# Attention outputs divided in the transposed layout, with reciprocals spread by DMA through HBM

## The chip, the cores and the metric

The kernel runs on one core of a Trainium2 chip. A core has a matrix engine (TensorE, "PE" in the profile; its weight loads are listed as "PEld"), three engines for elementwise work (VectorE "DVE", ScalarE "ACT", GpSimd "POOL"), a queue engine that only issues transfers (SyncE "SP"), and 16 DMA engines that carry the transfers. Each engine works through its own list of instructions in order, and waits at semaphores for the others. The metric is the device time of one execution in microseconds; lower is better. The median of three runs is compared.

## The reference

The input is x of 8 images x 512 tokens x 512 features, float32. The block is a half feed-forward, an attention, and a half feed-forward again, each on a layer-normalised input and added to x:

```python
x = x + 0.5 * ffn(layernorm(x), w_gate_up, w_proj)
x = x + attn(layernorm(x), Wq, Wk, Wv, Wo)
x = x + 0.5 * ffn(layernorm(x), w_gate_up, w_proj)
```

The feed-forward computes `silu(gate) * up` with ternary weights, normalises by the root mean square, and projects back. The attention has 32 heads of 16 features, and a sliding window: a query in a block of 128 tokens sees the keys of its own block and of the block before, at most 128 tokens back:

```python
scores = einsum('bhnrd,bhncd->bhnrc', qb, kw) * scale
scores = where(valid, scores, finfo(float32).min)
out = einsum('bhnrc,bhncd->bhnrd', softmax(scores), vw)
return out.reshape(B, T, D) @ Wo.T
```

The softmax's division can be done after the weighting: weight the values by the exponentials, sum the exponentials too, and divide the one by the other. The change is about where and in which layout this division is done.

## The kernel before

Three stages follow one another: the first feed-forward (tensors named `_a`), the attention (`_b`), the second feed-forward (`_c`). Intermediate rows go through HBM (`rows_a`, `rows_b`). SBUF memory of the attention is reused by the last stage's tiles, so some loads of its weights (`wgu`, `wp`) wait until attention tiles are released.

**The attention stage** (line 610 on). An image is cut in 4 chunks of 8 heads (`i` counts chunks over all images, 32 in all, `NJ` = 4 per image), and a chunk in 4 units of 128 tokens (`u` counts units, `t` is the unit in its chunk, 0 to 3). One pass of the loop at line 902 emits the work of one unit, in an order written out by hand for TensorE, VectorE, ScalarE and GpSimd; the order of SyncE's transfers is left to the scheduler. In a pass:

- `probabilities(u)`: scores in transposed form, keys on partitions (tile `sp`, line 798), turned into exponentials by ScalarE with one part on VectorE (lines 806 to 812, tile `pT`), and masked by GpSimd (line 817).
- `weighted(u - 1)`: the weighting (tile `av`, line 833). It needs the mask of the unit before. Its stationary operand is `vones`: for every head 32 columns, 16 of them the values, 16 of them ones. So `av` has, for each head, 16 rows of weighted values (numerators) and 16 rows that all hold the sum of the exponentials (denominators), in the transposed layout: features on partitions, tokens along the free dimension. There are 4 heads side by side in the 128 partitions, and two such halves `h`.
- `maxima(u + 6)`: scores in the other form (tile `sm`, line 750) and their row maxima on VectorE (line 758).
- projections, one per unit: values of the next image at t = 0 (`wv`), output of the last image at t = 1 (`wo`, `output(b - 1, j)`), queries and keys of chunk i + 3 at t = 2 and t = 3 (`wq`, `wk`). The query and key terms are rearranged over partitions by four transfers each on SyncE (lines 708 and 720).
- the division, every second unit, for two units together: ScalarE copies `av` to SBUF (tile `ab`, line 842); `turned` transposes it on TensorE (tile `abT`, line 851), tokens onto partitions; `divided` takes reciprocals of the denominators and multiplies on VectorE (lines 857 and 861, tile `o`); `turned_back`, one unit later, transposes back on TensorE (tile `oTp`, line 873), and ScalarE copies the result into `oT` (line 876), from which the output projection reads.

Pools set what can be in flight: `ps_s` has 6 PSUM buffers for scores and transposes, `ps_av` one and `ps_mm` one, `work` and `opool` hold the SBUF tiles.

Of the kernel before, what the change touches and what calls it, by code (L numbers as in the profile page):

```python
# [8 lines left out]
F32 = mybir.dt.float32  # L9
# [6 lines left out]
P = 128  # L16
# [8 lines left out]
def macaron_block(  # L25
# [63 lines left out]
    h_kept = [dram.tile([P, T], F32, name=f"h_kept{c}") for c in range(FC)]  # L89
    wp_kept = [dram.tile([P, 2, D], F32, name=f"wp_kept{u}") for u in range(FC // 2)]  # L90
# [519 lines left out]
    def attention_stage():  # L610
# [19 lines left out]
        opool = pool(s, "o_b", 7)  # L630
# [15 lines left out]
        for name, src in (("wv", wv_t), ("wq", wq_t), ("wk", wk_t), ("wo", wo_t)):  # L646
            attn_w[name] = fixed[name].tile([P, DC, D], F32, name=f"{name}_sb")
            nc.sync.dma_start(attn_w[name], src.rearrange("(c p) e -> p c e", p=P))
# [11 lines left out]
        for tile_ in vones:  # L660
            nc.gpsimd.memset(tile_[:, :, :, DK:], 1.0)
# [4 lines left out]
        abTs, qs, ks, ms, pTs, avs, abs_, os_, oTs = {}, {}, {}, {}, {}, {}, {}, {}, {}  # L666
# [57 lines left out]
        def values(b, t):  # L724
            rows = slice(t * P, (t + 1) * P)
            pairs = [(xss[b][:, k, rows], attn_w["wv"][:, k, :]) for k in range(DC)]
            sum_of_products(
                f"wv_{b}_{t}", pairs,
                lambda ps: nc.vector.tensor_copy(
                    vones[b % 2][:, t, :, :DK], ps.rearrange("p (h d) -> p h d", d=DK)  # L730
                ),
            )
# [90 lines left out]
        def weighted(u):  # L823
# [16 lines left out]
            if t % 2 == 1:  # L840
                abs_[i] = work.tile([P, 2, 2, P], F32, tag="ab", name=f"ab_{u}", bufs=2)
                nc.scalar.copy(abs_[i], avs.pop(i))

        def turned(u):

            i, t = u // TB, u % TB
            pt = abTs[i] = ps_s.tile([P, 2, 2, P], F32, tag="s", name=f"abT_{u}")
            ab = abs_.pop(i)
            for m in range(2):
                for h in range(2):  # L850
                    nc.tensor.transpose(pt[:, m, h, :], ab[:, h, m, :], ident)  # L851

        def divided(u):
            i, t = u // TB, u % TB
            rows = abTs.pop(i).rearrange("p m h (g r) -> p (m h) g r", r=32)
            rden = small.tile([P, 4, NG, 1], F32, tag="rden", name=f"rden_{u}")
            nc.vector.reciprocal(rden, rows[:, :, :, DK : DK + 1])
            os_[i] = work.tile([P, 2, 2, NG, DK], F32, tag="o", name=f"o_{u}", bufs=2)
            for m in range(2):
                for h in range(2):  # L860
                    nc.vector.tensor_tensor(
                        os_[i][:, m, h], rows[:, 2 * m + h, :, :DK],
                        rden[:, 2 * m + h].to_broadcast([P, NG, DK]), ALU.mult,
                    )

        def turned_back(u):
            i, t = u // TB, u % TB
            if t == 1:
                oTs[i] = opool.tile([P, T], F32, tag="oT", name=f"oT_{i}")
            o = os_.pop(i)  # L870
            back = ps_s.tile([P, 2, P], F32, tag="s", name=f"oTp_{u}")
            for m in range(2):
                nc.tensor.transpose(
                    back[:, m, :], o[:, m].rearrange("p h g d -> p (h g d)"), ident
                )
            nc.scalar.copy(
                oTs[i][:, (t - 1) * P : (t + 1) * P], back.rearrange("p m q -> p (m q)")
            )
# [23 lines left out]
        for u in range(-row - row // 2 - 2, units + row):  # L902
# [13 lines left out]
            if t == 0 and 0 <= b - 1 < B:  # L916
                residual_loaded(b - 1, j)
# [15 lines left out]
            if t == 1 and 0 <= b - 1 < B:  # L933
                output(b - 1, j)
# [46 lines left out]
```

## Time and profile before

| | |
|---|---|
| median of 3 runs | 2475.7 us (2471.64 to 2480.78) |
| span of the profiled execution | 2475.1 us (the page gives no time of its own around it; the median is 0.6 us above) |
| attention stage in the span | about 800 to 1730 us |
| one image of it, 4 chunks | 109 us |
| mean granted TensorE clock | 0.977 of full speed |
| `abT` transposes on TensorE | 256 matmul records (1% of the chain that ended last) |
| `oTp` transposes on TensorE | 128 matmul records |
| HBM read, written | 66.32 MB, 41.16 MB |

A line of the profile names the source line, the engine, the operation, what is written and read, the number of instructions, and the time. A bracket behind a line of the list in order of time is the idle time of the engine just ahead, and who ended it. "SPq" lines are the times in which SyncE issues transfers, not the transfers themselves; these have their own table of times from issue to landing. The granted clock is the share of full speed at which TensorE was allowed to run; 1.00 is full speed.

### The profile page before, as it was taken

The numbers are of one execution on the slowest core, as the hardware profiler recorded it, in microseconds if no ns is written. First come the engines' busy times: TensorE is split into PE (matmuls) and PEld (weight loads), VectorE is DVE, ScalarE is ACT, GpSimd is POOL, SyncE is SP. The second block draws the span as 40 slices with busy tenths as digits, with TensorE's granted clock in tenths as the row PEclk, the third lists the DMA queues.
The fourth block names the chain that finished last, engine by engine and source line by source line (L and its number), as shares of the span: only waits on it lengthen the run. The fifth ranks groups of instructions, "written<-read, shape, count | busy, mean of one in ns | idle before, by whom it ended". The sixth has DMA issues, their size and how long they took to land.

```text
span 2475.1 us, 43237 instructions
## 1 busy us (share of the span) xinstructions
PE 2387.1 (96%) x17208; PEld 1779.4 (72%) x17208; DVE 1339.8 (54%) x3929; ACT 982.2 (40%) x1476; POOL 862.8 (35%) x714
## 2 busy tenths in 40 slices
PE   5999999999999999999999999987899999999998
PEld 4778888888887456666666666654688888888887
DVE  7884444453444666766767676662444443453442
ACT  6773222222221355656566565654222222222221
POOL 0000444444445122223222223222345444444444
PEclk9899999999999989999999999988899999999999
DMA  4443100000011523333332333253100000000000
GB/s 161 145 145 129 42 35 1 34 35 1 35 52 34 145 53 87 101 79 88 81 105 74 93 81 83 74 166 125 68 35 1 35 35 1 35 34 1 35 17 17
DMA packets 63192, 160.58 MB, mean 65 GB/s; under 512 B 7440, under 2 KB 11536, under 8 KB 59920
## 3 DMA queue, kind: packets, MB, share of 16 engines
q1 hardware_dynamic: 47680, 116.68, 16.5%
q10 hardware_dynamic: 15312, 41.16, 4.4%
q8 instruction: 135, 2.21, 0.4%
q14 instruction: 65, 0.53, 0.1%
HBM read 66.32 MB, written 41.16 MB: 43 GB/s over the span
## 4 chain that ended last, share of the span: by engine, by line
PE 92%; DVE 3%; ACT 2%; issue 1%; DMA 0%; POOL 0%; ACTq 0%; POOLq 0%; DVEq 0%; SPq 0%
PE gu_c L281 19%; PE gu_a L281 18%; PE o_c L316 9%; PE o_a L316 9%; PE sp L798 5%; PE av L833 5%; PE wk L677 5%; PE wv L677 5%; PE wq L677 5%; PE wo L677 5%; PE sm L750 4%; PE abT L851 1%; PE neg L777 1%; PE ptn_b L225 1%; PE ptn_a L225 1%
## 5 line engine op out<-in xcount | busy, mean ns | idle before, releaser
L281 PE MATMUL gu_a<-xs_a,wgu_a 128*128 128x512 f32 x2048 | 497.8, 396 | 7.2 <-ACT sg_a L292 3.0
L281 PE MATMUL gu_c<-xs_c,wgu_c 128*128 128x512 f32 x2048 | 490.4, 392 | 0.7 <-ACT xs_c L228 0.7
L817 POOL TENSOR_SCALAR_AFFINE_SELECT pT<-pT 128x1024 f32<-128x1024 f32 x224 | 243.2, 1106 | 632.9 <-ACT pT L812 632.9
L281 PEld LDWEIGHTS gu_a<-xs_a,wgu_a 128*128 128x128 f32 x2048 | 387.2, 191 | 90.7 <-ACT sg_a L292 4.3
L281 PEld LDWEIGHTS gu_c<-xs_c,wgu_c 128*128 128x128 f32 x2048 | 383.3, 189 | 80.1 <-ACT xs_c L228 1.1
L758 DVE CUSTOM_DVE_ANT_0 seen<-sm,window 128x256 f32<-128x256 f32 (+1 forms) x1024 | 331.3, 387 | 86.6 <-PE sm L750 85.9
L316 PE MATMUL o_a<-wp_a,hs_a 128*128 128x512 f32 x1024 | 256.3, 395 | 0.0
L316 PE MATMUL o_c<-wp_c,hs_c 128*128 128x512 f32 x1024 | 251.6, 389 | 0.0
L297 DVE TENSOR_TENSOR h_c<-gu_c,sg_c 128x512 f32<-128x512 f32 x128 | 88.2, 689 | 276.8 <-PE gu_c L281 274.5
L587 POOL TENSOR_TENSOR sq_c<-h_c 128x512 f32<-128x512 f32 x120 | 125.0, 1042 | 316.4 <-DVE h_c L297 301.6
L810 ACT ACTIVATE pT<-sp 128x512 f32<-128x512 f32 (+1 forms) x384 | 181.2, 545 | 129.3 <-PE sp L798 129.3
L812 ACT ACTIVATE pT<-pT 128x2048 f32<-128x2048 f32 (+1 forms) x128 | 217.3, 1697 | 10.9 <-DVE pT L806 7.6
L316 PEld LDWEIGHTS o_a<-wp_a,hs_a 128*128 128x128 f32 x1024 | 192.7, 190 | 40.0 <-DVE hs_a L306 0.4
L316 PEld LDWEIGHTS o_c<-wp_c,hs_c 128*128 128x128 f32 x1024 | 192.2, 188 | 39.9
L297 DVE TENSOR_TENSOR h_a<-gu_a,sg_a 128x512 f32<-128x512 f32 x128 | 88.2, 689 | 234.7 <-PE gu_a L281 230.0
L588 POOL TENSOR_TENSOR ss_c<-ss_c,sq_c 128x512 f32<-128x512 f32 x120 | 192.2, 1602 | 8.9
L292 ACT ACTIVATE sg_c<-gu_c 128x512 f32<-128x512 f32 x128 | 76.6, 599 | 261.3 <-PE gu_c L281 248.2
L302 ACT CAST hs_c<-h_c 128x512 fp32r<-128x512 f32 x128 | 79.4, 621 | 252.7 <-DVE h_c L297 252.7
L587 POOL TENSOR_TENSOR sq_a<-h_a 128x512 f32<-128x512 f32 x90 | 94.2, 1047 | 229.7 <-DVE h_a L297 220.7
L306 DVE TENSOR_TENSOR hs_c<-h_c,hs_c 128x512 fp32r<-128x512 f32 x128 | 124.1, 970 | 83.1 <-ACT hs_c L302 83.1
L292 ACT ACTIVATE sg_a<-gu_a 128x512 f32<-128x512 f32 x128 | 76.4, 597 | 214.8 <-PE gu_a L281 203.2
L302 ACT CAST hs_a<-h_a 128x512 fp32r<-128x512 f32 x115 | 71.3, 620 | 202.0 <-DVE h_a L297 199.6
(137 smaller groups left out, 3129.1 us busy)
## 6 DMA issues: line engine op xcount, KB each, us to landing
ks<-k SPq DMA_DIRECT2D x128, 256.0 KB, 4.8
qs<-q SPq DMA_DIRECT2D x128, 128.0 KB, 2.4
wf_gu<-w_gate_up_dram SPq DMA_DIRECT2D x16, 512.0 KB, 3.6
wgu_kept<-wgu_a ACTq DMA_DIRECT2D x16, 512.0 KB, 2.7
rows_a<-x_a ACTq DMA_DIRECT2D x8, 1024.0 KB, 4.0
x_b<-rows_a SPq DMA_DIRECT2D x8, 1024.0 KB, 5.5
xr<-rows_a ACTq DMA_DIRECT2D x32, 256.0 KB, 5.4
rows_b<-xr SPq DMA_DIRECT2D x32, 256.0 KB, 2.1
```

The lines of the kernel that those rows point to most:

```text
L281: nc.tensor.matmul(ps, wgu[c][:, i * DC + k, :], xss[b][:, part, k, :], start=(k == 0 and part == 0), stop=(k == DC - 1 and part == 1),)
L292: nc.scalar.activation(sg, gate, AF.Silu)
L297: nc.vector.tensor_tensor(h, up, sg, ALU.mult)
L302: nc.scalar.copy(hs[:, 0, :], h)
L316: nc.tensor.matmul(ops[t], hs[:, part, t * P : (t + 1) * P], wp[e // 2][:, e % 2, :], start=(e == begin and part == 0), stop=(e == end and ...
L587: nc.gpsimd.tensor_tensor(sq, h, h, ALU.mult)
L588: nc.gpsimd.tensor_tensor(sumsq, sumsq, sq, ALU.add)
L677: nc.tensor.matmul(ps, lhs, rhs, start=(n == 0), stop=(n == len(pairs) - 1))
L758: nc.vector.tensor_tensor_reduce(out=seen[:, : n * P], in0=tiles[g][:, h, : n * P], in1=window[:, (2 - n) * P :], scale=-1.0, scalar=3.4e3 ...
L810: nc.scalar.activation(under, tiles[g][:, :, : n * P], AF.Relu, scale=-1.0)
L812: nc.scalar.activation(seen, seen, AF.Exp, scale=-1.0)
L817: nc.gpsimd.affine_select(out=half, in_=half, compare_op=ALU.is_ge, fill=0.0, base=0, pattern=[[0, 2 * NG], [sign, P]], channel_multiplier ...
```

## The change

Nothing is transposed any more for the division; it is done in the layout that the weighting leaves.

- For heads with `h` = 0 the values stand in the even columns of `vones` and ones in the odd ones; for `h` = 1 the other way round. So numerators and denominators alternate over partitions. `values` writes the columns by two copies, and the memset covers the whole of `vones`.
- ScalarE copies `av` into `sums` (the copy of line 842, a tile over the whole chunk).
- At t = 0 of the next chunk, `denominators` stores one denominator row per head to HBM (two transfers) and loads them back as 128 partitions x 32 (one transfer); `gathered` copies the numerators of `h` = 1 over the denominators of `h` = 0 (one transfer), so that one tile holds all numerators.
- At t = 2, `inverted` takes reciprocals on VectorE, stores them to HBM (one transfer) and reads every row back onto the 16 partitions of its head (eight transfers). All of these are on SyncE's queue.
- At t = 3, `divided` multiplies on GpSimd, into `oT`.
- The output projection and its residual load come one chunk later, the loop runs four units longer, `oT` has 8 buffers instead of 7, and `wo` is loaded with its rows interleaved, by two transfers.

```diff
--- before.py
+++ after.py
@@ -87,6 +87,8 @@
     rows_b = [dram.tile([P, TB, D], F32, name=f"rows_b{b}") for b in range(B)]
     wgu_kept = [dram.tile([P, 2 * DC, P], F32, name=f"wgu_kept{c}") for c in range(FC)]
     h_kept = [dram.tile([P, T], F32, name=f"h_kept{c}") for c in range(FC)]
+    dens = [dram.tile([2, NG, T], F32, name=f"dens{n}") for n in range(2)]
+    inverses = [dram.tile([2, NG, T], F32, name=f"inverses{n}") for n in range(2)]
     wp_kept = [dram.tile([P, 2, D], F32, name=f"wp_kept{u}") for u in range(FC // 2)]
 
     PSUM = bass.MemoryType.PSUM
@@ -627,7 +629,7 @@
         }
         ring = pool(s, "ring_b", 3)
         probs = pool(s, "probs_b", 3)
-        opool = pool(s, "o_b", 7)
+        opool = pool(s, "o_b", 8)
         work = pool(s, "work_b", 3)
 
         ps_s = pool(s, "ps_s", 6, PSUM)
@@ -645,7 +647,14 @@
         attn_w = {}
         for name, src in (("wv", wv_t), ("wq", wq_t), ("wk", wk_t), ("wo", wo_t)):
             attn_w[name] = fixed[name].tile([P, DC, D], F32, name=f"{name}_sb")
-            nc.sync.dma_start(attn_w[name], src.rearrange("(c p) e -> p c e", p=P))
+            if name != "wo":
+                nc.sync.dma_start(attn_w[name], src.rearrange("(c p) e -> p c e", p=P))
+                continue
+            by_half = src.rearrange("(c h r) e -> h r c e", h=2, r=P // 2)
+            for h in range(2):
+                nc.sync.dma_start(
+                    attn_w[name].rearrange("(r two) c e -> r two c e", two=2)[:, h], by_half[h]
+                )
         vones = [
             fixed[f"vones{i}"].tile([P, TB, N_HEADS, 2 * DK], F32, name=f"vones{i}_sb")
             for i in range(2)
@@ -658,12 +667,12 @@
         for h in range(2):
             nc.vector.tensor_copy(selects[h], max_rows[h].to_broadcast([P, P]))
         for tile_ in vones:
-            nc.gpsimd.memset(tile_[:, :, :, DK:], 1.0)
+            nc.gpsimd.memset(tile_, 1.0)
         for tile_ in terms_of_negs:
             nc.gpsimd.memset(tile_.bitcast(F32), 0.0)
 
         xrs = {}
-        abTs, qs, ks, ms, pTs, avs, abs_, os_, oTs = {}, {}, {}, {}, {}, {}, {}, {}, {}
+        qs, ks, ms, pTs, avs, sums, dens_sb, oTs = {}, {}, {}, {}, {}, {}, {}, {}
         NJ = DC
         units = B * NJ * TB
 
@@ -724,12 +733,15 @@
         def values(b, t):
             rows = slice(t * P, (t + 1) * P)
             pairs = [(xss[b][:, k, rows], attn_w["wv"][:, k, :]) for k in range(DC)]
-            sum_of_products(
-                f"wv_{b}_{t}", pairs,
-                lambda ps: nc.vector.tensor_copy(
-                    vones[b % 2][:, t, :, :DK], ps.rearrange("p (h d) -> p h d", d=DK)
-                ),
-            )
+
+
+            def kept(ps):
+                heads = vones[b % 2][:, t].rearrange("p (j h g) d -> p h j g d", h=2, g=NG)
+                made = ps.rearrange("p (j h g d) -> p h j g d", h=2, g=NG, d=DK)
+                for h in range(2):
+                    nc.vector.tensor_copy(heads[:, h, :, :, h::2], made[:, h])
+
+            sum_of_products(f"wv_{b}_{t}", pairs, kept)
 
         def scores_tile(name):
             return [
@@ -838,44 +850,46 @@
                         )
 
             if t % 2 == 1:
-                abs_[i] = work.tile([P, 2, 2, P], F32, tag="ab", name=f"ab_{u}", bufs=2)
-                nc.scalar.copy(abs_[i], avs.pop(i))
-
-        def turned(u):
-
-            i, t = u // TB, u % TB
-            pt = abTs[i] = ps_s.tile([P, 2, 2, P], F32, tag="s", name=f"abT_{u}")
-            ab = abs_.pop(i)
-            for m in range(2):
-                for h in range(2):
-                    nc.tensor.transpose(pt[:, m, h, :], ab[:, h, m, :], ident)
-
-        def divided(u):
-            i, t = u // TB, u % TB
-            rows = abTs.pop(i).rearrange("p m h (g r) -> p (m h) g r", r=32)
-            rden = small.tile([P, 4, NG, 1], F32, tag="rden", name=f"rden_{u}")
-            nc.vector.reciprocal(rden, rows[:, :, :, DK : DK + 1])
-            os_[i] = work.tile([P, 2, 2, NG, DK], F32, tag="o", name=f"o_{u}", bufs=2)
-            for m in range(2):
-                for h in range(2):
-                    nc.vector.tensor_tensor(
-                        os_[i][:, m, h], rows[:, 2 * m + h, :, :DK],
-                        rden[:, 2 * m + h].to_broadcast([P, NG, DK]), ALU.mult,
+                if t == 1:
+                    sums[i] = work.tile([P, 2, T], F32, tag="sums", name=f"sums_{i}", bufs=2)
+                nc.scalar.copy(
+                    sums[i][:, :, (t - 1) * P : (t + 1) * P],
+                    avs.pop(i).rearrange("p h m q -> p h (m q)"),
+                )
+
+        def rows_of(t, h):
+
+            return t.rearrange("(r two) t -> r two t", two=2)[:, h]
+
+        def denominators(i):
+
+            for h in range(2):
+                nc.sync.dma_start(
+                    dens[i % 2][h],
+                    sums[i][:, h].rearrange("(g r) t -> g r t", r=32)[:, 1 - h],
+                )
+            den = dens_sb[i] = work.tile([P, T // DK], F32, tag="den", name=f"den_{i}", bufs=1)
+            nc.sync.dma_start(den, dens[i % 2].rearrange("h g (s e) -> (h g s) e", s=DK))
+
+        def gathered(i):
+
+            nc.sync.dma_start(rows_of(sums[i][:, 0], 1), rows_of(sums[i][:, 1], 1))
+
+        def inverted(i):
+            inv = work.tile([P, T // DK], F32, tag="inv", name=f"inv_{i}", bufs=1)
+            nc.vector.reciprocal(inv, dens_sb.pop(i))
+            nc.sync.dma_start(inverses[i % 2].rearrange("h g (s e) -> (h g s) e", s=DK), inv)
+            oTs[i] = opool.tile([P, T], F32, tag="oT", name=f"oT_{i}")
+            for h in range(2):
+                rows = rows_of(oTs[i], h)
+                for g in range(NG):
+                    nc.sync.dma_start(
+                        rows[DK * g : DK * (g + 1)],
+                        inverses[i % 2][h, g].unsqueeze(0).to_broadcast([DK, T]),
                     )
 
-        def turned_back(u):
-            i, t = u // TB, u % TB
-            if t == 1:
-                oTs[i] = opool.tile([P, T], F32, tag="oT", name=f"oT_{i}")
-            o = os_.pop(i)
-            back = ps_s.tile([P, 2, P], F32, tag="s", name=f"oTp_{u}")
-            for m in range(2):
-                nc.tensor.transpose(
-                    back[:, m, :], o[:, m].rearrange("p h g d -> p (h g d)"), ident
-                )
-            nc.scalar.copy(
-                oTs[i][:, (t - 1) * P : (t + 1) * P], back.rearrange("p m q -> p (m q)")
-            )
+        def divided(i):
+            nc.gpsimd.tensor_tensor(oTs[i], sums.pop(i)[:, 0], oTs[i], ALU.mult)
 
         def residual_loaded(b, t):
             xrs[b, t] = work.tile([P, D], F32, tag="xr", name=f"xr_{b}_{t}")
@@ -899,7 +913,7 @@
             mybir.EngineType.Pool,
         }
         s.enter_context(tc.manual_schedule(engines=engines))
-        for u in range(-row - row // 2 - 2, units + row):
+        for u in range(-row - row // 2 - 2, units + row + TB):
             i, t = u // TB, u % TB
             b, j = i // NJ, i % NJ
             if b == -2 and j == 2:
@@ -913,8 +927,9 @@
                 probabilities(u)
             if 0 <= u - 1 < units:
                 weighted(u - 1)
-            if t == 0 and 0 <= b - 1 < B:
-                residual_loaded(b - 1, j)
+            out_b, out_t = divmod(i - NJ - 1, NJ)
+            if t == 0 and 0 <= out_b < B:
+                residual_loaded(out_b, out_t)
             ended = u - 1 + AHEAD
             if 0 <= ended < units and ended % TB == TB - 1:
 
@@ -930,19 +945,22 @@
                 values(0, 2 * (j - 2) + t)
             if t == 0 and 0 < b + 1 < B:
                 values(b + 1, j)
-            if t == 1 and 0 <= b - 1 < B:
-                output(b - 1, j)
+            if t == 1 and 0 <= out_b < B:
+                output(out_b, out_t)
             if t == 2 and 0 <= i + 3 < B * NJ:
                 queries(i + 3)
             if t == 3 and 0 <= i + 3 < B * NJ:
                 keys(i + 3)
             if j == 2 and 0 < b + 2 < B:
                 norms[b + 2][2](t)
-            if 0 <= u - 1 < units and (u - 1) % 2 == 1:
-                turned(u - 1)
-                divided(u - 1)
-            if 0 <= u - 2 < units and (u - 2) % 2 == 1:
-                turned_back(u - 2)
+            if 0 <= i - 1 < B * NJ:
+                if t == 0:
+                    denominators(i - 1)
+                    gathered(i - 1)
+                if t == 2:
+                    inverted(i - 1)
+                if t == 3:
+                    divided(i - 1)
             if j == 0 and t == 3 and 0 < b + 2 < B:
                 row_loaded(b + 2)
         s.close()
```

## The prediction

> **What bounds the kernel now.** I read the busy times of the page first, then the table by stretches to find the stage the change touches, then one chunk in order of time on each engine, then the landing times of the transfers, and last the places where TensorE waits today.
>
> ```profile
> PE 2387.1 (96%) x17208; PEld 1779.4 (72%) x17208; DVE 1339.8 (54%) x3929; ACT 982.2 (40%) x1476; POOL 862.8 (35%) x714
> ```
> ```profile
> 1179.00:1288.00 109.00, 108.80 (x1297) 66.43 (x1297) 76.01 (x360) 64.91 (x96) 31.48 (x29) 1.00 0.34 88
> ...
> 1615.00:1720.00 105.00, 87.03 (x1125) 57.66 (x1126) 50.48 (x241) 60.11 (x87) 30.04 (x28) 0.84 0.39 124
> ```
> The second fence has, per stretch, the busy times of TensorE, its weight loads, VectorE, ScalarE and GpSimd, then the granted clock and the DMA share. One image of the attention (four chunks) takes 109 us, and TensorE is busy for all of it at full clock; every other engine has a third or more free. So TensorE's instruction list is the bound there, and time removed from it is time won as long as nothing makes it wait. In the stage's last 105 us it already waits.
>
> ```profile
> 1227.24 0.60 PE L851 MATMUL abT<-ident,ab 128*128 128x128 f32 x4
> 1227.77 0.45 PE L798 MATMUL sp<-qs,ks 32*128 32x128 f32 x8
> 1234.17 0.38 PE L873 MATMUL oTp<-ident,o 128*128 128x128 f32 x2
> 1234.48 0.51 PE L798 MATMUL sp<-qs,ks 32*128 32x256 f32 x8
> 1241.12 0.60 PE L851 MATMUL abT<-ident,ab 128*128 128x128 f32 x4
> 1242.56 0.65 PE L833 MATMUL av<-pT,vones_sb 128*32 128x128 f32 x16
> ```
> These are the ends of the units of one chunk on TensorE (start, length). `abT` holds the list from 1227.24 to 1227.77 (0.53) and `oTp` from 1234.17 to 1234.48 (0.31); the last line is the first weighting of the next chunk.
>
> ```profile
> 1227.44 0.60 ACT L690 ACTIVATE q<-wq 128x512 fp32r<-128x512 f32 x1 [1.13 <-PE wq L677]
> 1228.07 0.69 DVE L691 SCALAR_TENSOR_TENSOR q<-wq,q 128x512 fp32r<-128x512 f32 x1 [2.01 <-ACT q L690]
> 1228.68 0.25 DVE L857 RECIPROCAL rden<-abT 128x16 f32<-128x16 f32 x1
> 1228.63 2.38 SPq L708 DMA_DIRECT2D qs<-q  x4
> 1235.72 3.14 SPq L720 DMA_DIRECT2D ks<-k  x4
> 1237.16 1.91 ACT L812 ACTIVATE pT<-pT 128x2048 f32<-128x2048 f32 x1
> 1239.14 2.32 POOL L817 TENSOR_SCALAR_AFFINE_SELECT pT<-pT 128x1024 f32<-128x1024 f32 x2 [3.55 <-ACT pT L812]
> ```
> The same chunk elsewhere. The query terms end at 1228.76 and their copies leave SyncE from 1228.63; the exponentials of the next chunk's first unit end at 1239.07, and GpSimd masks them from 1239.14 (2.32; the median pair takes 2.14) until 1241.46. The weighting at 1242.56 needs this mask: the slack is 1.1 us here, and 0.5 us in the tightest unit (mask ends 1221.20, weighting 1221.69).
>
> ```profile
> qs<-q SPq DMA_DIRECT2D x16, 128.0 KB, 2.4
> xr<-rows_a ACTq DMA_DIRECT2D x4, 256.0 KB, 5.4
> rows_b<-xr SPq DMA_DIRECT2D x4, 256.0 KB, 2.1
> ```
> KB and microseconds from issue to landing: nothing today is as small as the new transfers.
>
> ```profile
> L587 POOL TENSOR_TENSOR sq_c<-h_c 128x512 f32<-128x512 f32 x120 | 125.0, 1042 | 316.4 <-DVE h_c L297 301.6
> L588 POOL TENSOR_TENSOR ss_c<-ss_c,sq_c 128x512 f32<-128x512 f32 x120 | 192.2, 1602 | 8.9
> ```
> GpSimd's product of a tile with itself takes 1.04 us, its sum of two different tiles 1.60 us.
>
> ```profile
> 948.33 0.80 PE L798 MATMUL sp<-qs,ks 32*128 32x256 f32 x6 [1.17 <-ACT oT L876]
> 949.90 1.90 PE L833 MATMUL av<-pT,vones_sb 128*32 128x128 f32 x32
> ```
> ```profile
> 948.00:952.00 4.00, 3.67 (x62) 3.01 (x66) 2.04 (x11) 2.37 (x6) 2.14 (x2) 0.57 0.01 2
> ```
> What a short wait costs: after 1.17 us for `oT` the granted clock is 0.57 over the next 4 us, and 32 weightings take 1.90 us where they take 1.08 elsewhere.
>
> **The change, part by part.** A is the time at which a chunk's query projection leaves TensorE's list (1227.24 above).
>
> *Removed from TensorE:* two `abT` groups and two `oTp` groups per chunk, 2 x (0.53 + 0.31) = 1.68 us. They are in the bounding list, so this is a gain of 1.68 per chunk where nothing else ends later.
>
> *Removed elsewhere:* reciprocals and products on VectorE (2 x 0.87) and two copies of 0.37 on ScalarE. Both engines have free time, so I count nothing. The value copy becomes two; by the 128x256 form of L806 (0.41 each) against 0.69 that is 0.13 more, hidden under the same free time, and 0.13 if that were gone. The copy of the numerators keeps its 0.57.
>
> *Added on SyncE, per chunk:* 13 issues: two stores of denominators, one gathering copy, one load, one store of reciprocals, eight row copies. At 0.46 us each (three weight loads at 1653.97 took 1.38) this is 6 us, plus three waits for a landing of about 2.1, on top of today's 5.9: some 18 of 25.5 us, so the queue does not fill. Traffic grows by 0.45 MB on 2.3 MB per chunk, the DMA share from 0.34 to about 0.40. What is queued behind: the key copies go out from about A+9.9 instead of A+8.5, land 3.1 + 5.1 later, near A+18, and their first reader (`sm` in the next chunk's third unit) comes near A+21. Hidden, with 3 us to spare; a later landing costs its excess once per chunk. The query copies have a chunk of room, the row stores longer. Splitting the load of `wo` (808.8, first used at 972) and the extra oT buffer cost nothing.
>
> *Added wait, the step that decides.* In the built program SyncE has, per chunk, the reciprocal store, one row copy, the four query copies, then the other seven row copies. GpSimd has the division between the mask of a chunk's last unit and that of the next chunk's first, so a late row copy holds that mask, and behind it TensorE's weighting. Worked out from A:
> - query terms on VectorE end: 1.52; reciprocal 0.25 (it stands behind them): 1.77
> - store of reciprocals lands, by `rows_b` 2.1: 3.87 (the first row copy waits for it)
> - its issue 0.46, four query copies 2.38, six more issues 2.76: the last row copy leaves at 9.47
> - its landing, by the query copies 2.4: 11.87
> - division of two different tiles 1.60: 13.47
> - mask 2.14, to the matmul 0.10: the weighting can start at 15.71.
> TensorE gets there on its own at 15.32 - 0.46 (a normalisation transpose in this chunk) - (0.53 + 0.31 + 0.53) = 13.49. So it waits 2.2 us per chunk. Low end: landings of 2.0 (the smallest in that group), issues of 0.33, division 1.04: 13.74, a wait of 0.25; transfers this small may land faster still, so the end is 0, and a wait cannot be negative. High end: store 2.9 (as among the weight loads), issues 0.79 (key copies, 3.14/4), landing 5.4 (`xr`, also read from HBM), division 1.60: 21.8, a wait of 8.3. I take the values of the nearest rows, 2.2.
> [...]
>
> *Clock after that wait.* The fence's wait of 1.17 us lost 4 x 0.43 = 1.7 us; the one at 889.33 (also 1.17) lost 8 x 0.43 = 3.4 (clock 0.57 from 890 to 898); one of 2.44 at 1619 lost about 1.7 and one of 2.44 at 1646 nothing; one of 0.90 at 844 nothing (the next `wq` ran in 3.60). I take 1.5 for a wait of 2.2; ends 0 and 3.4.
> [...]
>
> *Steady part:* 2.2 + 1.5 - 1.68 = +2.0 per chunk; 26 chunks with a full next unit give 52, less 6 x 0.46 where a normalisation transpose gives cover: **+50**. Break-even is a wait of 1.68 with no loss of clock.
>
> *Head:* the memset of a values tile covers 128x4096 instead of 128x2048 (1.81 us at 792.20, ahead of the last squares on GpSimd, for which TensorE then waits until 802.28): +1.8, ends 0 and 3.6.
>
> *End of the stage:* after the last weighting (1713.86) the outputs start at 1715.06 today. Then come copy 0.57, store 2.1, load 3.0 (between 2.4 and 5.4), reciprocal 0.25, store 2.1, eight issues 3.7, landing 2.4, division 1.6 = 15.7, and some 3 for five loads of `wp` between them (0.5 MB each, at the 410 GB/s of 1658 to 1662): 18.7 instead of 1.2, **+17.5** (14 to 25). In the last four chunks TensorE waits 17.2 us for `ab` and the transposes take 6.7: up to 24 to win, of which the chain of ScalarE and GpSimd keeps a part; I take half, **-12** (-24 to 0). In chunk 29 the row copies queue behind 11 loads of `wgu` (5.6 MB, 14 us): **+7** (0 to 14). Together +12.5, ends -10 and +39.
>
> **Sum:** 2475.1 (the span; the median of the runs is 0.6 above it, the page has nothing around it) + 50 + 1.8 + 12.5 = 2539.
>
> **Rivals.**
> 1. *The row copies land in time* (wait at most 0.9, no loss of clock): for it the low end and the quiet 0.90 us wait; against it, six issues alone span 2.8 us and two landings stand in series. 26 x (0 to 0.9 - 1.68) = -44 to -20, +14: **2446 to 2469**. This is the other side; it decides once the last row copy lands before about A+10.
> 2. *Wait and gain cancel* (1 to 2.2 us of wait, clock undisturbed, as after the 2.44 us wait at 1646): 26 x (-0.7 to +0.5) + 14: **2471 to 2502**.
> 3. *Row copies land like `xr`* (5.4, sixteen readers of one row): wait 5.2, clock 1.5: 26 x 5.0 + 20: **2625**. Against: 32 KB is an eighth of `xr`.
> 4. *The key copies get late* and `sm` waits: only if issues take over 0.8 us; then 2 to 3 us per chunk more: **2590 to 2620**.
>
> **How the numbers follow.** Forecast (wait 1.2 to 4 us with some loss of clock, 2502 to 2595) 0.56; rival 1 0.18; rival 2 0.12; rival 3 0.08; rival 4 0.06. Half a percent (12 us) is about what a measurement of this kernel tells from no change. Faster (under 2463): most of rival 1, 0.16; same (2463 to 2488): the rest of it and half of rival 2, 0.08; slower 0.76. The range leaves out half of rival 1 and the far part of rivals 3 and 4: 2458 to 2605; the forecast's own is 2502 to 2595.
>
> **What would show it.** PE count 17208 - 384; a group `av` with an idle time put down to GpSimd, about 2 us in the second unit of each chunk; GpSimd's division waiting on DMA until about A+12, and its mask right behind it; a clock below 1.00 in the stretches 960 to 1615; 114 to 118 us per image instead of 109; TensorE resuming the last stage some 18 us after the last weighting plus the outputs. I am wrong if `av` has no wait, if the division has a length near 1.0, or if the clock stays at 1.00 behind waits of 2 us.

## The result and the profile after

The changed kernel takes 2550.1 us (median of 4 runs, 2548.6 to 2555.1) against 2475.1 us before in the same sitting: a ratio of 1.0306, with a 95% interval of 1.0288 to 1.0323. The profiled execution has a span of 2547.5 us, 72.4 us more than before, and a mean granted clock of 0.963 instead of 0.977. The prediction was 2539 us, slower.

The page's busy line, and its group of weightings (count of instructions, then busy time and mean, then the idle time of TensorE just before them and who ended it):

```profile
PE 2358.8 (93%) x16824; PEld 1732.1 (68%) x16824; DVE 1297.4 (51%) x3673; ACT 961.9 (38%) x1412; POOL 901.2 (35%) x746
L845 PE MATMUL av<-pT,vones_sb 128*32 128x128 f32 x3584 | 132.7, 287 | 95.0 <-POOL pT L829 91.1
```
The 384 transposes are gone from TensorE, and its busy time is 28 us less. But it now stands idle for 95.0 us in front of weightings, 91.1 of them put down to GpSimd's mask. Before, that column read 0.8.

Two stretches of the attention stage, with the columns of the earlier fence (busy time of TensorE, weight loads, VectorE, ScalarE and GpSimd; clock; DMA share):

```profile
1188.00:1308.00 120.00, 109.36 (x1249) 63.48 (x1249) 70.31 (x326) 62.50 (x88) 35.84 (x33) 0.93 0.35 95
1663.00:1766.00 103.00, 72.84 (x1037) 45.41 (x1030) 42.22 (x198) 55.24 (x77) 34.72 (x32) 0.82 0.39 122
```
TensorE is no longer busy all the time in the middle of the stage, and its clock there is 0.93, where it was 1.00. VectorE and ScalarE are busy for a smaller share than before (59% and 52% of the stretch instead of 70% and 60%), and GpSimd for 35.84 of 120 us, so none of them has become the bound by its amount of work.

One chunk in order of time, the counterpart of the chunk in the prediction. A, the end of the query projection, is 1213.95 here:

```profile
1214.06 0.60 ACT L699 ACTIVATE q<-wq 128x512 fp32r<-128x512 f32 x1 [1.13 <-PE wq L686]
1214.69 0.69 DVE L700 SCALAR_TENSOR_TENSOR q<-wq,q 128x512 fp32r<-128x512 f32 x1 [2.83 <-ACT q L699]
1215.29 0.34 DVE L880 RECIPROCAL inv<-den 128x32 f32<-128x32 f32 x1
1215.66 0.32 SPq L881 DMA_DIRECT2D inverses<-inv  x1
1217.29 0.56 SPq L886 DMA_DIRECT2D oT<-inverses  x1
1217.95 2.45 SPq L717 DMA_DIRECT2D qs<-q  x4
1220.44 4.98 SPq L886 DMA_DIRECT2D oT<-inverses  x7
1227.13 1.27 POOL L892 TENSOR_TENSOR oT<-sums,oT 128x512 f32<-128x512 f32 x1 [8.91 <-DMA oT<-inverses]
1228.37 2.13 POOL L829 TENSOR_SCALAR_AFFINE_SELECT pT<-pT 128x1024 f32<-128x1024 f32 x2
1229.51 1.07 PE L845 MATMUL av<-pT,vones_sb 128*32 128x128 f32 x16 [1.89 <-POOL pT L829]
```
Reciprocal, its store, one row copy, the four query copies, seven more row copies, and only then the division, for which GpSimd has stood idle 8.91 us. The mask is next in GpSimd's list; the exponentials that it masks ended at 1224.85, but it starts when the division ends. The weighting starts after the first of the two masks, and TensorE has waited 1.89 us.

The end of the stage:

```profile
1765.72 6.28 PE L686 MATMUL wo<-wo_sb,oT 128*128 128x512 f32 x14
1775.77 0.32 SPq L881 DMA_DIRECT2D inverses<-inv  x1
1780.59 4.95 SPq L886 DMA_DIRECT2D oT<-inverses  x8
1787.37 1.26 POOL L892 TENSOR_TENSOR oT<-sums,oT 128x512 f32<-128x512 f32 x1 [18.85 <-DMA oT<-inverses]
1788.68 13.44 PE L686 MATMUL wo<-wo_sb,oT 128*128 128x512 f32 x26 [16.69 <-POOL oT L892]
```
The last weighting ends at 1765.78. One output and three quarters of the next can be done with what is there (14 matmuls); then TensorE waits 16.69 us for the last division.

The difference of the two spans can be put together from marks on TensorE. In both traces I took the starts of the key projections `wk` of chunks 7 and 31 (before 986.4 and 1637.1, after 983.2 and 1687.9), which stand 24 chunks apart in the steady part, the end of the last weighting, and the first transpose of the last stage, `ptn_c`:

| stretch | before | after | difference |
|---|---|---|---|
| start of the span to the key projection of chunk 7 | 986.4 | 983.2 | -3.2 |
| 24 chunks in the steady part | 650.7 | 704.7 | +54.0 |
| from there to the end of the last weighting | 76.8 | 77.9 | +1.1 |
| last weighting to the last stage's first transpose | 26.5 | 46.2 | +19.8 |
| last stage | 734.8 | 735.5 | +0.7 |

So three quarters of the loss are in the steady part, 2.25 us per chunk, and one quarter at the end.

### The profile page after: what moved, and what is told of

Same layout as the page of the kernel before. It is cut to its first block, busy times and chain, and to the rows that moved or that the text cites. A ratio compares the mean times of both kernels' runs of the same rounds, so it can differ in the third digit from the quotient of the medians.

```text
span 2547.5 us, 42955 instructions
## 1 busy us (share of the span) xinstructions
PE 2358.8 (93%) x16824; PEld 1732.1 (68%) x16824; DVE 1297.4 (51%) x3673; ACT 961.9 (38%) x1412; POOL 901.2 (35%) x746
## 4 chain that ended last, share of the span: by engine, by line
PE 77%; DMA 6%; SPq 5%; DVE 5%; POOL 3%; issue 2%; ACT 2%; POOLq 0%; ACTq 0%; DVEq 0%
PE gu_c L283 18%; PE gu_a L283 17%; PE o_c L318 9%; PE o_a L318 9%; PE wo L686 5%; PE wq L686 4%; SPq L886 3%; PE av L845 3%; PE sm L762 3%; PE sp L810 2%; PE wk L686 2%; DMA oT<-inverses 2%; DMA ks<-k 2%; DMA inverses<-inv 2%; POOL oT L892 1%
## 5 line engine op out<-in xcount | busy, mean ns | idle before, releaser
L845 PE MATMUL av<-pT,vones_sb 128*32 128x128 f32 x3584 | 132.7, 287 | 95.0 <-POOL pT L829 91.1
L845 PEld LDWEIGHTS av<-pT,vones_sb 128*32 128x32 f32 x3584 | 94.1, 113 | 115.0 <-POOL pT L829 99.3
```

The source lines that it names most:

```text
L845: nc.tensor.matmul(avs[i][32 * g : 32 * g + 32, h, t % 2, :], vones[b % 2][:, block, NG * (2 * j + h) + g, :], pTs[u - t + block][:, 2 * g ...
```

## The experiments

The theory: the change's instructions and transfers cost nothing by themselves in the steady part. What costs is that the row copies land late and that the division waits for them in front of a mask in GpSimd's order; and a part of the loss is the granted clock, 0.93 in the stretch above where it was 1.00. Rivals: GpSimd's own 1.27 us for the division; the added transfers or the strided copies slowing engines down. All experiments start from the changed kernel. Of the runs that follow, the table has the time, the ratio to the kernel before with its interval, the 24 chunks of the table above, what TensorE waited for GpSimd's masks in them, and the time from the last weighting to `ptn_c`, all in us:

| run | time | ratio | 24 chunks | waits for masks | end |
|---|---|---|---|---|---|
| before | | | 650.7 | 0 | 26.5 |
| the change | 2550.1 | 1.0306 (1.0288 to 1.0323) | 704.7 | 66.7 | 46.2 |
| divide_later | 2455.5 | 0.9942 (0.9920 to 0.9963) | 620.6 | 0.6 | 46.2 |
| two_row_copies | 2460.1 | 0.9947 (0.9926 to 0.9968) | 624.7 | 3.1 | 44.7 |
| no_spread | 2425.2 | 0.9812 (0.9797 to 0.9827) | 613.2 | 0.6 | 28.8 |
| sixteen_row_copies | 2706.3 | 1.0954 (1.0935 to 1.0973) | 824.8 | 166.4 | 50.3 |
| invert_earlier | 2439.4 | 0.9839 (0.9817 to 0.9860) | 613.7 | 0 | 43.4 |
| early_two_copies | 2439.5 | 0.9847 (0.9813 to 0.9881) | 613.3 | 0.6 | 43.3 |
| early_two_tail_on_act | 2439.3 | 0.9830 (0.9806 to 0.9855) | 613.5 | 0.6 | 44.1 |
| outputs_three_later | 2439.8 | 0.9848 (0.9830 to 0.9867) | 617.4 | 0.6 | 42.5 |
| outputs_two_later | 2433.9 | 0.9822 (0.9800 to 0.9844) | 613.4 | 1.0 | 41.5 |

### The division behind the mask

```diff
+            if t == 0 and 0 <= i - 2 < B * NJ:
+                divided(i - 2)
             if 0 <= i - 1 < B * NJ:
...
-                if t == 3:
-                    divided(i - 1)
```

> The division of a chunk is emitted at t = 0 of the chunk after next, behind the masks of that pass, instead of one pass earlier; nothing else moves, and the same instructions run. Theory: the late row copies cost time only because the division stands in front of a mask in GpSimd's order. Then the 24 weightings of chunks 4 to 27 that waited for GpSimd (64.8 us in all) wait no more, the granted clock of the attention goes back to 1.00 (some 28 us more), and the last stage's end is unchanged: 2550 - 65 - 28 = about 2457 us, an image at about 102 us. Rival 1: it is GpSimd's own time for the division (1.27 us) that delays a mask, wherever it stands; then the wait moves to the second unit of the chunk, about 0.8 us each, and the time is about 2490. Rival 2: the added transfers or the strided copies slow the engines themselves; then the time stays near 2550.

Measured: 2455.5 us, 94.6 less than the change with the same instructions. The stretch 960 to 1615 of the changed kernel and of this one:

```profile
960.00:1615.00 655.00, 592.87 (x6947) 343.85 (x6940) 390.35 (x1805) 349.61 (x491) 200.72 (x185) 0.95 0.36 95
```
```profile
960.00:1615.00 655.00, 647.07 (x7897) 381.86 (x7897) 440.82 (x2040) 395.95 (x555) 228.72 (x207) 1.00 0.40 107
```
TensorE is busy for 647 of 655 us instead of 593, and its clock is back at 1.00. Nothing was taken away; the division only stands behind one more mask. That excludes rival 2 as the main cause, and rival 1 too: GpSimd spends the same 1.27 us, and the waits did not move to another unit (0.6 us in 24 chunks). A small wait is new: TensorE waited 2.4 us in those chunks, and 1.8 before them, for key copies, which leave SyncE after the row copies.

### Fewer row copies, and more

```diff
-                for g in range(NG):
-                    nc.sync.dma_start(
-                        rows[DK * g : DK * (g + 1)],
-                        inverses[i % 2][h, g].unsqueeze(0).to_broadcast([DK, T]),
-                    )
+                nc.sync.dma_start(
+                    rows,
+                    inverses[i % 2][h].unsqueeze(1).to_broadcast([NG, DK, T]),
+                )
```

> Each half's four row copies become one transfer onto 64 partitions: two issues instead of eight, the same bytes; the division stays where it is. Theory: the last row copy leaves SyncE about 6 x 0.7 = 4.2 us earlier, so nearly all of the mean wait of 2.70 us goes (the longest was 4.29), the clock comes back, and the tail is 4 us shorter: about 2455 us. Rival 1: the issues are not what makes the copies late, but the landing of all these bytes: a transfer of 128 KB lands 2 to 3 us later than one of 32 KB, a wait of about 1.2 us per chunk remains, and the time is about 2500. Rival 2 (traffic or strided copies slow the engines): about 2545.

Measured: 2460.1 us. With the division in its old place, taking six issues out of SyncE's list removes all but 3.1 of the 66.7 us of waits. The issues were what made the copies late; that one transfer now carries four times the bytes did not bring the wait of 1.2 us per chunk that the first rival expected. The 24 chunks still take 11.5 us more than in the run without transfers below; 3.1 of them are these waits and 2.7 are waits for other data (`xn_b`, `pT`), and what makes up the rest was not tested.

The opposite, every row copy in two:

```diff
+                    for e in range(0, DK, DK // 2):
                         nc.sync.dma_start(
-                            rows[DK * g : DK * (g + 1)],
-                            inverses[i % 2][h, g].unsqueeze(0).to_broadcast([DK, T]),
+                            rows[DK * g + e : DK * g + e + DK // 2],
+                            inverses[i % 2][h, g].unsqueeze(0).to_broadcast([DK // 2, T]),
                         )
```

> Every row copy is cut in two, onto 8 partitions each: 16 issues instead of 8, the same bytes; the division stays where it is. Theory: the last row copy leaves SyncE 8 x 0.65 = 5.2 us later, and since TensorE already waits in every chunk, all of it is added: the wait of the weighting grows from 2.70 to about 7.9 us, chunks 4 to 27 cost 24 x 5.2 = 125 us more, and the time is about 2675 us, more if the clock falls further. Rival (the wait is not on SyncE's issues): 2550 to 2570.

Measured: 2706.3 us, 31 more than expected, and slower as the theory has it. The groups of weightings of the two runs, fewer copies first:

```profile
L845 PE MATMUL av<-pT,vones_sb 128*32 128x128 f32 x3584 | 131.3, 284 | 21.0 <-POOL pT L829 16.9
```
```profile
L845 PE MATMUL av<-pT,vones_sb 128*32 128x128 f32 x3584 | 141.9, 300 | 222.7 <-POOL pT L829 219.1
```
With 2, 8 and 16 copies the idle time in front of weightings is 21, 95 and 223 us. The 24 chunks take 120.1 us longer, near the 125 expected: the mean wait went from 2.78 to 6.93 us, 4.15 more instead of 5.2, and the clock, priced below, made up for most of the difference. What the expectation left out are the chunks outside these 24: 13.3 us ahead of them, 16.8 after them, and 4.0 at the end.

### The change without its transfers

```diff
-        def denominators(i):
...
-        def inverted(i):
...
         def divided(i):
-            nc.gpsimd.tensor_tensor(oTs[i], sums.pop(i)[:, 0], oTs[i], ALU.mult)
+            both = sums.pop(i)
+            oTs[i] = opool.tile([P, T], F32, tag="oT", name=f"oT_{i}")
+            nc.gpsimd.tensor_tensor(oTs[i], both[:, 0], both[:, 1], ALU.mult)
```

> Left out: denominators, reciprocals and all the transfers of the division. GpSimd multiplies the two halves of the sums by each other instead, so its 1.27 us and its place stay, and the result is not the attention's. It prices the new layout without its transfers. Theory: without the row copies the division starts at once, the waits and the loss of clock go (65 + 28 us), and the end of the stage has no chain through HBM: 16.7 us at the last output shrink to about 2. About 2550 - 93 - 16 = 2441 us; chunks 4 to 27 take about 25.4 us each. Rival 1 (GpSimd's own 1.27 us is the cost): the waits stay at 1 us and above, about 2490. Rival 2 (strided copies, new layout): about 2530.

Measured: 2425.2 us, 16 less than expected, since the chunks outside the 24 gained too (5.1 us ahead of them, 9.2 after). This is the floor for the layout: 24 chunks in 613.2 us, 25.55 each, against 27.11 before. So the new layout is worth **1.56 us per chunk**, and with it the other numbers per chunk fall out. Not all of it is transposes: the kernel before has one wait of 2.44 us for `ab` in these chunks (ahead of 1619.10), with the clock at half for 3.41 us behind it; without these 4.1 us it is 1.39. The change itself lost 704.7 - 613.2 = 91.5 us to this floor, 3.81 per chunk. The waits for masks are 66.7 of it, 2.78 per chunk; the rest, **1.03 per chunk**, is work at a lower clock. The 24 chunks of the changed kernel and of this run show it, with the clock ahead of the DMA share:

```profile
983.22:1687.94 704.72, 636.81 (x7466) 368.35 (x7465) 417.06 (x1936) 372.76 (x525) 214.06 (x197) 0.95 0.35 94
```
```profile
978.09:1591.33 613.24, 611.42 (x7468) 358.26 (x7464) 414.57 (x1911) 372.59 (x525) 217.16 (x197) 1.00 0.35 91
```
The same matmuls keep TensorE busy for 25.4 us longer, at a clock of 0.95 instead of 1.00. With sixteen copies the same sum gives 211.6 us, of which 166.4 are waits and 45.2, or 1.88 per chunk, clock.

Two rows show what such a rest consists of: the same query projection in the run with the division put later and in the run of the next section.

```profile
947.84 0.45 PE L762 MATMUL sm<-ks,qs 32*128 32x128 f32 x8 [1.83 <-DMA ks<-k]
948.71 5.29 PE L686 MATMUL wq<-xs_b,wq_sb 128*128 128x512 f32 x8
```
```profile
945.40 3.60 PE L686 MATMUL wq<-xs_b,wq_sb 128*128 128x512 f32 x8
```
Behind a wait of 1.83 us (and one of 0.47 just ahead of it) the same eight matmuls take 5.29 us instead of 3.60, and from 862 to 982 the granted clock is 0.94 in the first run and 0.97 in the second. This wait of 1.83 us was followed by 1.69 us of slower work.

### The chain earlier

```diff
-                if t == 2:
+                if t == 1:
                     inverted(i - 1)
```

> Reciprocals, their store and the eight row copies are emitted at t = 1 instead of t = 2, some 6.4 us earlier; the division stays in front of the mask. In SyncE's order all eight row copies then stand ahead of the query copies. Theory (a late landing holds the mask): the reciprocal can start at about A - 5.8 (the load of the denominators left SyncE 12 us before A in the chunk read), the store lands 1.6 later and the last of eight row copies leaves 5.6 after that and lands by about A + 4.5, seven microseconds before GpSimd comes to the division. No weighting waits for GpSimd in chunks 4 to 27, and the time is that of the division put later, 2455 us, or some 3 us less if the key copies, which leave earlier too, no longer hold the maxima's scores (3.2 us there). Rival (the division's place in front of the mask costs something even when its data are there): 1.27 us of GpSimd less the slack of 0.5 to 1.1, so 0.2 to 0.8 per chunk, 2460 to 2475. Rival 2: the denominators are not there yet at t = 1 and VectorE waits for them, 2 us a chunk: about 2500.

Measured: 2439.4 us, 16 less than with the division put later, and 39 less than the kernel before. In this run, around one division, SyncE and GpSimd:

```profile
1226.97 4.97 SPq L886 DMA_DIRECT2D oT<-inverses  x8
1232.05 2.96 SPq L717 DMA_DIRECT2D qs<-q  x4
1233.46 1.09 POOL L829 TENSOR_SCALAR_AFFINE_SELECT pT<-pT 128x1024 f32<-128x1024 f32 x1 [3.01 <-ACT pT L824]
1234.52 1.28 POOL L892 TENSOR_TENSOR oT<-sums,oT 128x512 f32<-128x512 f32 x1
```
All eight row copies have left at 1231.94, in one group ahead of the query copies, and the division at 1234.52 starts right behind the mask, with no idle time ahead of it. It stands where it stood in the change, in front of the next chunk's mask, and holds nothing up there: in the 24 chunks no weighting waits for GpSimd, and TensorE waits 1.4 us in all, none of it for GpSimd or a transfer. They take 613.7 us, 0.5 more than without any transfers, so the transfers by themselves cost next to nothing. VectorE did not wait for the denominators. Both rivals fall.

Against the division put later the spans differ by 18.2 us: 6.9 in the 24 chunks, 6.6 before them, 4.7 after them. In the steady part 3.6 of the 6.9 are waits that are gone, most of them for key copies; the other 3.7 are busy time of TensorE (611.4 us instead of 615.1) at a clock of 1.00 in both runs, and nothing here explains them. Ahead of the steady part, 5.6 of the 6.6 are lost between the key projections of chunks 0 and 7, where the fences above show a wait of 1.83 and a projection 1.69 longer. I had put all this at 3 us, since I counted the 3.2 us of waits and neither the clock nor the end.

Together with two row copies:

> The reciprocals at t = 1 and two row copies instead of eight, together. Theory: in the steady part neither leaves anything to win for the other, so chunks 4 to 27 take what one alone gives, about 25.4 us each; only the end of the stage, where nothing covers the chain, is shorter by the issues, some 4 us: about 2450 us. Rival: the two add up in the steady part too (SyncE's queue itself delays the key copies): about 2440.

Measured: 2439.5 us, the same as with the first edit alone. That is the rival's number, but not for its reason: the steady part has nothing left to win (613.3 against 613.7), as the theory said, and it was the theory's starting point, 2455 us, that was too high. The gain at the end was not there: 43.3 us from the last weighting to `ptn_c` instead of 43.4.

### The end of the stage

```diff
+        def queue_of(i):
+            return nc.scalar if i == B * NJ - 1 else nc.sync
...
-                nc.sync.dma_start(
+                queue.dma_start(
                     dens[i % 2][h],
```

All transfers of the last chunk's division, the gathering copy too, go out through `queue_of(i)`.

> As the reciprocals at t = 1 with two row copies, and the transfers of the very last chunk's division go out on ScalarE's queue instead of SyncE's, so that no load of the last stage's weights stands between them. Theory (SyncE's order lengthens the last chain): from the end of the last weighting, copy 0.7, two stores 1.1 and a landing of 2, load 0.5 and 2, reciprocal 0.4, store 0.3 and 1.6, two row copies 1.2 and 2.4, division 1.3, four outputs 14.5: 28 us to the last output product instead of 34.7 with two row copies, and 6.5 us off the time, about 2443 us. Rival (the transfers land late because the weight loads fill the DMA engines, in whatever queue they are issued): no change, about 2450.

Measured: 2439.3 us, no change. ScalarE's queue, GpSimd and TensorE at the end of this run, then two stretches of it, the end and one in the steady part (clock, DMA share and GB/s last):

```profile
1666.81 0.33 ACTq L886 DMA_DIRECT2D inverses<-inv  x1
1672.45 1.18 ACTq L890 DMA_DIRECT2D oT<-inverses  x2
1679.46 1.26 POOL L896 TENSOR_TENSOR oT<-sums,oT 128x512 f32<-128x512 f32 x1 [18.19 <-DMA xr<-rows_a]
1680.77 9.45 PE L686 MATMUL wo<-wo_sb,oT 128*128 128x512 f32 x17 [12.67 <-POOL oT L896]
```
```profile
1660.00:1680.00 20.00, 8.10 (x14) 3.02 (x13) 1.04 (x2) 0.32 (x1) 1.81 (x2) 0.67 0.77 256
1214.00:1234.00 20.00, 19.92 (x237) 11.88 (x236) 15.46 (x68) 13.63 (x18) 7.72 (x7) 1.00 0.35 94
```
No load stands between the store and the row copies any more, yet the row copies leave 5.64 us after the store's issue, where it was 1.63 in the chunk shown above, and the division starts 5.8 us after the last of them has left. (The list puts the end of GpSimd's wait down to `xr<-rows_a`, a load on the same queue; the division reads `oT`, not `xr`.) In those 20 us the DMA engines are busy for 0.77 of the time with 256 GB/s, against 0.35 and 94 in the steady part: the weights of the last stage are being loaded. The edit did not take these loads out of the way: five of them leave SyncE from 1666.65 on, beside the store, and from 1671.1 to 1679.3, which takes in the row copies, the DMA engines are busy for at least 0.9 of every slice of 0.55 us. So SyncE's order between these transfers is not what makes them late; that the traffic of the loads does fits the rows, but no run took the loads away, so it is argued and not shown. Of the 13.96 us that TensorE waited at the end of the run with SyncE's queue alone, 12.67 remain with ScalarE's.

What covers the end is work. The outputs can come later still, so that products of the image before stand in the wait:

```diff
-        opool = pool(s, "o_b", 8)
+        opool = pool(s, "o_b", 9)
...
-            out_b, out_t = divmod(i - NJ - 1, NJ)
+            out_b, out_t = divmod(i - NJ - 2, NJ)
```

with the loop four units longer; this is two chunks later, and the other run has `i - NJ - 3`.

> The same with outputs two chunks later and 9 buffers: by the theory one more product of 3.6 us in the wait, about 2436 us; by the rival 2437 to 2442.

> As the reciprocals at t = 1 with two row copies; the output products come three chunks later than before the change instead of one (oT has 9 buffers), so three outputs of the image before, not one, stand between the last weighting and the outputs that need the last division. Theory (the 14 us at the end are an uncovered wait for transfers): two more products of 3.6 us fill 7.2 us of it, the wait falls from 14.0 to about 7, and chunks 28 to 31 are shorter by as much as the end has more to do: 2439 - 7 = about 2432 us. Rival (each weight load or row store that SyncE puts ahead of the last row copies lengthens the chain by as much): the wait stays and the time with it, 2437 to 2442.

Measured: 2433.9 and 2439.8 us. TensorE at the end of the run with two:

```profile
1650.83 10.63 PE L686 MATMUL wo<-wo_sb,oT 128*128 128x512 f32 x22
1669.99 13.01 PE L686 MATMUL wo<-wo_sb,oT 128*128 128x512 f32 x26 [8.53 <-POOL oT L891]
```
Eight more matmuls stand in front of the wait, and it is 8.53 us instead of 13.96. With three it is 6.2. The step of two is 5.6 us faster by the medians, where the theory has 3.6, but the intervals of the two ratios overlap; the step of three lost in its profile part of what it won, since a normalisation came late there (3.71 and 0.77 us of waits for `xn_b` between the key projections of chunks 8 and 9, which stand 30.5 us apart instead of 26.7 to 27.7). Why it came late isn't settled.

The version with outputs two chunks later is the fastest that was run with nothing left out: 0.9822 of the kernel before (0.9800 to 0.9844). The single edit of one line, reciprocals at t = 1, gives 0.9839.

## Why the prediction was right

The forecast of 2539 us, slower, held: 2550. The steps, against what was measured:

- **Transposes removed, 1.68 per chunk:** 1.56 by the run without transfers, 1.39 without the old wait for `ab` and its clock. Right, and a little high.
- **The wait, 2.2 per chunk:** 2.78 on average (0.96 to 4.85). Right in mechanism and place: the weighting of a chunk's first unit, held by the mask, which the division holds. Its terms erred in both directions. To the low side: the issue of a row copy was counted at 0.46 us, from weight loads, and the seven in a row take 4.98, 0.71 each. They end at A + 11.5; an issue takes 0.59 in the median, so the last one begins at A + 10.9, and the sum had it at A + 9.5. To the high side: the first row copy could follow 1.6 us behind the store instead of 2.1, the division took 1.27 instead of 1.60, and the weighting needs only the first of the two masks, 1.07 and not 2.14. The landing of the last copy was right: the division starts 2.3 us after its issue begins, counted at 2.4. Result: weighting at A + 15.56 in the chunk shown, predicted A + 15.71. That the two agree is luck: errors of about 2 us each way cancelled.
- **Clock, 1.5 per chunk:** 1.03 on average. Right in sign and too high. The traces of the two kernels show more than this mean. In them the granted clock is either 1.00 or 0.50; its half stretches in the attention stage last 3.41 us or a multiple of it, and in one trace they all begin on the same raster (in the changed kernel at 997.5, 1055.5, 1113.5 and 1171.5, each 17 times 3.41 us apart, and so on). The length of a wait alone did not settle what it cost: of the changed kernel's 24 waits for masks in the 24 chunks, 17 are shorter than such a stretch (0.96 to 3.32 us), and nine of these have one (begun during the wait or less than 2 us behind it) and eight have none; the seven longer ones (3.47 to 4.85) all have one. Two stretches of the changed kernel, the first behind a wait of 1.56 us, the second behind one of 3.13 (the clock stands ahead of the DMA share):

```profile
1171.50:1174.90 3.40, 3.40 (x5) 1.33 (x4) 2.45 (x16) 0.30 (x1) 2.13 (x2) 0.51 0.81 242
1350.50:1353.90 3.40, 3.40 (x37) 1.95 (x38) 2.07 (x13) 0.44 (x1) 3.06 (x3) 1.00 0.29 85
```
- **Steady part, +50:** +54.0 in 24 chunks, 2.25 each by the terms 2.78 + 1.03 - 1.56. Right.
- **Head, +1.8:** the larger memset did cost, +2.5 us: from the start of the first stage's last group `o_a` to the first `ptn_b` it is 12.84 us instead of 10.31, with 5.63 instead of 3.92 us of waiting. But the first stage reached that point 3.6 us earlier in this execution (788.36 against 791.97), and in others at 789.97 and 790.86, with the same code there. That difference is one between executions, and a difference of spans carries it along.
- **End of the stage, +12.5:** +20.8 (1.1 and 19.8). The chain through HBM was put at +17.5 and cost 19.8. The +7 for row copies behind the loads of `wgu` came: one weighting there waited 8.60 us for a mask, because the row copies left 8.9 us after the store of the reciprocals, with the DMA engines busy all the time (share 1.00, 394 GB/s from 1711 to 1721):

```profile
1711.77 0.32 SPq L881 DMA_DIRECT2D inverses<-inv  x1
1712.18 2.27 SPq L574 DMA_DIRECT2D wgu_c<-wgu_kept  x2
1720.68 4.97 SPq L886 DMA_DIRECT2D oT<-inverses  x8
```
What failed is the -12 for waits on `ab` that go. From the key projection of chunk 31 to the last weighting TensorE waits 24.3 us instead of 14.8, and besides the 8.60 its weightings wait for masks and for `sums` instead of for `ab`. Old waits were replaced, not removed.

Of the rivals, the first (row copies in time, 2446 to 2469) is the time that the change takes when its division moves by one pass: 2455. The fourth (key copies late) appeared in that same run, at 4.2 us in all and not 2 to 3 per chunk.

## What to carry over

Work was moved here off the bounding engine onto a chain of transfers, and in the steady part the price was not the chain's length but where its last consumer stood in GpSimd's list: look at what is queued behind the instruction that waits, and give the chain a pass more, before cutting anything. The same instructions cost 75 us or won 39 us, by one line. Count issues on the queue at the rate of their own kind (the prediction's 0.46 us for a row copy, from weight loads, was 0.71 in the chunk shown), and add the clock: waits of 2.78 us on average cost TensorE another 1.03 us each in slower work. At the end of the stage, where nothing covered the chain, work put off to fill it cut the wait from 13.96 to 8.53 us; another queue for the same transfers left 12.67.

## What the hardware showed that I had not expected

- One broadcast transfer from HBM onto 64 partitions, 128 KB written, did the work of four of 32 KB, and what TensorE saw of its landing was small: waits for masks fell from 66.7 to 3.1 us.
- A 16 KB store to HBM let its follower start 1.6 us after its issue in the steady chunk shown (DMA share 0.39) and 5.6 us in the stretch where the DMA engines were 0.77 busy.
- In the changed kernel GpSimd's product of two different tiles took 1.26 to 1.29 us in all 32 cases, where its sum of two different tiles in the other stages took 1.62 in the median. But 11 of those 210 sums took 1.28 too, so the operation alone did not settle it.
- From the changed kernel to the one with sixteen row copies the clock's price grew less than the wait: 1.03 us per chunk at a mean wait of 2.78, 1.88 at 6.93. In the first, 16 half stretches fall in the 24 chunks; in the second, the 16 weightings behind each of the 24 waits take 1.08 us, where they take 0.65 behind the wait of 3.13 us shown above.
